# A two-layer graph network on one core: own pools for the staging tiles of the transformed taps, and another order for the first loads of the neighbour parts

## The chip, the cores and the metric

The kernel runs on one core of a Trainium2 chip. Its metric is the device time of one execution in microseconds. TensorE (PE), VectorE (DVE), ScalarE (ACT), GpSimd (POOL) and SyncE (SP) each work through their own list of instructions in order; SP and POOL also issue the DMAs, each to a queue of its own (q1 for SP, q0 for POOL in the profile).

## The reference, cut to what matters

128 graphs of 128 nodes with 256 channels go through two layers. The change lies in the first half of layer 0:

```
h = relu(layernorm(x))
xc = transpose(h)                                   # channels first
c  = relu(bn1(conv1x1(xc)))
c  = bn2(conv1d(c, conv2_w, 17 taps, pad 8))
x_conv = relu(c + xc)
s = h @ w_se.T + b_se                               # 3 channels
A = exp(-|s_n - s_m|^2) * adj
x_nmp = A @ relu(h @ w_msg.T + b_msg)               # the neighbour parts
layer 0 = GRU-like gates of (x_conv, x_nmp, h)
```

The convolution with 17 taps is done by a Fourier transform: the data and the taps are transformed, multiplied frequency by frequency, and transformed back.

## The kernel before, in words

All graphs are taken in 32 groups `q` of 4 graphs, and in two batches of 16 groups. The instruction order of every engine is written out by a small planner (`Order`, `Lane`) at build time: programs written as Python generators say at each `yield` how much time they think they have used, and the planner picks which one goes on. Nothing is reordered after that.

The stages that matter here, for the first batch, are these.

- `stage_a(q)` (lines 389 to 442) normalises a group, transposes it (`ph`, line 410), stores the transposed `hTa` into the DRAM tensor `hTd[q]` (line 415, a DMA that POOL issues), does the 1x1 convolution (`pc`, line 421) and the forward transform (`pf`, line 432) into the big on-chip tile `X`. `X` data is loaded by SP (`load_x`, line 381).
- `tap_weights()` (lines 459 to 499) runs beside it. It transforms the taps of the 17-tap convolution (`pw`, line 474), copies the results out of PSUM into a staging tile `ws` of 16 KB per partition (lines 479 and 481), and stores every `ws` into the DRAM tensor `wfd` with four DMAs of 320 KB issued by POOL (line 486). There are 16 `ws` tiles, named `ws{n}_{m}`, m even; the last four are `ws3_0`, `ws3_2`, `ws3_4`, `ws3_6`. They rotate through three buffers in the pool `tw`.
- When it is through, `tap_weights` closes `tw` (line 488) and opens the pools `wg`, `io`, `xe` and `fr` in the space that becomes free (lines 489 to 497). They have `reuse_waits="tile"`: a new tile waits for the last users of those old tiles whose bytes it covers, and for no others. `wmsg` and `bmsg`, the message weights and bias, are loaded at once by SP (lines 498 and 499).
- `early(q)` (lines 662 to 675) makes the neighbour part of group q: `load_n(q)` (lines 571 to 576) has SP load `hT` from `hTd[q]` and the adjacency `ad`; then `neighbours` (from line 608) does the embedding (`pse`, line 614), the messages (`pm`, line 630), the distances and the transposed adjacency (`pd`, lines 643 and 645) and the sum over neighbours (`px`, line 656).
- `stage_b(bat)` (lines 502 to 566) multiplies frequency by frequency (`pa`, `pb`, line 526). It starts with loads of `wf` from `wfd` (line 512), which SP issues behind the loads above, and which need every store of `wfd` to have landed. The neighbour parts are spread between its products.

On PE's list the end of `stage_a`, the first two neighbour parts, the messages of the third and then the first product of `stage_b` follow each other. On SP's list, after the last `x` load of the first batch (`xa15`), stand `wmsg`, `bmsg`, `hT0`, `adj0`, `hT1`, `adj1`, then `hT2`, `adj2` (which reuse buffers of group 0) and the first six loads of `wf`. On POOL's list stand the stores of `ws3_2`, of `hTd13`, of `ws3_4`, of `hTd14`, of `ws3_6`, of `hTd15`, and then the first store of a neighbour part.

In bytes per partition, from the built program: `tw` held `wse` at 23584, two `wt` tiles (taps as loaded) at 24128 and 40512, `wide` at 56896 and the three `ws` buffers at 58944, 75328 and 91712. The new pools put `hT0` at 55840 and `wmsg` at 80416.

Of the kernel before, what the change touches and what calls it, by code (L numbers as in the profile page):

```python
# [9 lines left out]
FP = mybir.dt.float32  # L10
# [5 lines left out]
B, N, D = 128, 128, 256  # L16
# [3 lines left out]
P = 128  # L20
# [187 lines left out]
def kernel(ctx: ExitStack, tc: tile.TileContext, x, adj, consts, vecs, w_se, conv1_w,  # L208
                    conv2_w, w_msg, b_msg, w_ih, w_hh, W1, W2, b2, fusion_w, out):
    nc = tc.nc  # L210
# [11 lines left out]
    hTd = [dr.tile([P, 2, 512], FP, name=f"hTd{q}") for q in range(NQ)]  # L222
# [10 lines left out]
    def c(name):  # L233
        a, b = CAT[name]
        return cst[:, a:b]
# [14 lines left out]
    def load_late():  # L250

        nc.sync.dma_start(out=fus, in_=fusion_w.partition_broadcast(P))
        nc.sync.dma_start(out=wse, in_=w_se.rearrange("(k p) o -> p k o", p=P))
        nc.sync.dma_start(out=cst[:, CFIRST:], in_=consts[:, CFIRST:])
# [76 lines left out]
    def fold_embedding():  # L331

        nc.vector.memset(wse9, 0.0)
        for role in range(3):
            nc.vector.tensor_copy(wse9[:, :, 3 * role:3 * role + 3], wse[:, :, :3])
        pbs = ptmp.tile([P, 512], FP, tag="tmp", name="pbs")
        nc.tensor.matmul(pbs[:, :1], c("sel"), v("b_se"), start=True, stop=True)
        bse = cp.tile([P, 1], FP, name="bse")
        nc.vector.tensor_copy(bse, pbs[:, :1])
        nc.vector.scalar_tensor_tensor(embb, emb[:, 4:8], bse, emb[:, 8:12],  # L340
                                       op0=ALU.mult, op1=ALU.add)
        yield 1.5, 0.0
# [26 lines left out]
    LATE, XA, MOM = {}, {}, {}  # L369
# [73 lines left out]


    mid, near = ExitStack(), ExitStack()
    tw = mid.enter_context(tc.tile_pool(name="tw", bufs=2))
    wse = tw.tile([P, 2, 67], FP, tag="wse", name="wse", bufs=1)
    wts = []

    def load_taps(n, *engines):  # L450

        wt = tw.tile([P, 16, D], FP, tag="wt", name=f"wt{n}")
        src = conv2_w.rearrange("(r n i) t o -> n t r i o", r=4, n=4)[n]
        for r in range(4):
            engines[r % len(engines)].dma_start(out=wt[32 * r:32 * r + 16], in_=src[:16, r])
        engines[0].dma_start(out=wt[16::32], in_=src[16])
        wts.append(wt)

    def tap_weights():

        yield 0.0, 16.0
        for n in range(4):
            for m in range(8):
                if m == (0 if n else 3) and n < 3:
                    load_taps(n + 1, nc.sync, nc.gpsimd)
                if (n, m) == (1, 3):
                    load_late()
                if m % 2 == 0:
                    ws = tw.tile([P, 4, 4, D], FP, tag="ws", name=f"ws{n}_{m}", bufs=3)
                pws = [(pgat if r < 3 else ptmp).tile([P, 2, D], FP, tag="gat" if r < 3 else "tmp",  # L470
                                                      name=f"pw{n}_{m}_{r}") for r in range(4)]
                for r in range(4):
                    rows = slice(32 * r, 32 * r + TAPS)
                    nc.tensor.matmul(pws[r][:F], c("tap")[rows], wts[n][rows, 2 * m:2 * m + 2],  # L474
                                     start=True, stop=True)
                i = m % 2 * 2
                for r in range(4):
                    if r < 2 or (r == 2 and m % 2):
                        nc.scalar.activation(ws[:F, r, i:i + 2], pws[r][:F], AF.Copy)
                    else:  # L480
                        nc.vector.tensor_copy(ws[:F, r, i:i + 2], pws[r][:F])
                yield 0.9, 2.2
                if m % 2:
                    for r in range(4):
                        i0 = 64 * r + 16 * n + 2 * (m - 1)
                        nc.gpsimd.dma_start(out=wfd[:, i0:i0 + 4], in_=ws[:F, r])
        yield from fold_embedding()
        mid.close()
        wg = ctx.enter_context(tc.tile_pool(name="wg", bufs=1, reuse_waits="tile"))
        LATE["wrz"] = wg.tile([P, 7, 3, D], FP, name="wrz")  # L490
        LATE["wn"] = wg.tile([P, 7, 2, P], FP, name="wn")
        LATE["wh"] = wg.tile([P, 7, 1, P], FP, name="wh")
        LATE["io"] = near.enter_context(tc.tile_pool(name="io", bufs=2, reuse_waits="tile"))
        LATE["xe"] = near.enter_context(tc.tile_pool(name="xe", bufs=1, reuse_waits="tile"))
        LATE["fr"] = near.enter_context(tc.tile_pool(name="fr", bufs=1, reuse_waits="tile"))
        LATE["wmsg"] = LATE["fr"].tile([P, 2, D], FP, name="wmsg")
        LATE["bmsg"] = LATE["fr"].tile([P, D], FP, name="bmsg")
        nc.sync.dma_start(out=LATE["wmsg"], in_=w_msg.rearrange("(k p) o -> p k o", p=P))
        nc.sync.dma_start(out=LATE["bmsg"], in_=b_msg.partition_broadcast(P))


    def stage_b(bat):
# [65 lines left out]

    EN, IN, IN2, X1, E_DONE, F_DONE = {}, {}, {}, {}, set(), set()

    def load_n(q):
        hT = LATE["io"].tile([P, 2, 512], FP, tag="hT", name=f"hT{q}")
        nc.sync.dma_start(out=hT, in_=hTd[q])
        ad = LATE["io"].tile([P, GB, N], FP, tag="adj", name=f"adj{q}")
        nc.sync.dma_start(out=ad, in_=adj[q * GB:(q + 1) * GB].rearrange("b n m -> n b m"))
        return hT, ad
# [85 lines left out]
    def early(q):  # L662

        while q not in A_DONE:
            yield 0.0, 0.5
        if q not in EN:
            EN[q] = load_n(q)
            yield 0.0, 6.0
        hT, ad = EN.pop(q)
        if q + 1 < NQ and q + 1 in A_DONE:  # L670
            EN[q + 1] = load_n(q + 1)
        xm = LATE["fr"].tile([P, 2, 512], FP, tag="xnmp", name=f"xnmp{q}", bufs=2)
        yield from neighbours(q, hT, ad, xm)
        nc.gpsimd.dma_start(out=xmd[q], in_=xm)
        E_DONE.add(q)
# [37 lines left out]
    def stage_c(q):  # L713
# [60 lines left out]
        for ps, i in ((p6, 5), (p5, 4)):  # L774
            part(ps, wrz, i, early, True, False)
            yield 1.75, 0.0
# [350 lines left out]
    load_xa(2)  # L1127
    fold()
    beside = Lane([tap_weights()] + [early(q) for q in range(NQ)])
    gates = Lane([fold_gates(), fold_fusion()], weight=0.5)  # L1130
    for bat, (during_a, during_b) in enumerate(((0.66, 0.5), (0.2, 0.65))):
# [60 lines left out]
```

## Time and profile before

| | |
|---|---|
| time, median of 3 runs | 2035.58 us (2028.67 to 2042.47) |
| the profiled execution's own time | 2034.12 us |
| its span, first to last instruction | 2032.3 us |
| PE busy | 1989.3 us, 98% of the span |
| DVE, POOL, ACT busy | 1285.2, 741.2 and 683.8 us |
| DMA | 281.91 MB, mean 139 GB/s |
| mean granted TensorE clock | 0.994 |

A busy PE is a PE with a matmul in it; the granted clock tells how fast it may run. In a timeline a line gives the start, the busy time, the engine, the source line, what is written and read, and in square brackets the idle time just before with what ended it. Stretches of time are given in microseconds from the span's start.

### The profile page before, as it was taken

What the parts mean: (1) busy time and instruction counts of PE and PEld (TensorE: products, weight loads), DVE (VectorE), ACT (ScalarE), POOL (GpSimd) and SP (SyncE); (2) the same over time, 40 slices, a digit from 0 to 9 for tenths busy, and PEclk for the clock granted to TensorE, in tenths of its full rate; (3) what the DMA queues carried; (4) which work ended last, traced back from release to release, by engine and by line L of the source; (5) the groups of instructions that cost most, each with busy time, mean ns of one, the idle gap of its engine ahead of it and who ended that gap; (6) DMA issues with size and microseconds to landing.
All of it is one profiled execution on the core that took longest, in us unless ns stands there. A gap on an engine that the chain in (4) does not pass through costs nothing.

```text
span 2032.3 us, 34053 instructions
## 1 busy us (share of the span) xinstructions
PE 1989.3 (98%) x12852; PEld 1653.7 (81%) x12852; DVE 1285.2 (63%) x2807; ACT 683.8 (34%) x1547; POOL 741.2 (36%) x898
## 2 busy tenths in 40 slices
PE   7998999999999999999999999999999999999998
PEld 5666888889888888778788878878888888878875
DVE  6774445785433566766775775677577757766643
ACT  4663222454222344232322322232233322232233
POOL 3542666332655022532333233224323323332330
PEclk9999999999999999999999999999999999999999
DMA  9987879744877633432322322322232323232121
GB/s 214 297 266 226 269 255 285 222 145 161 269 257 254 188 115 89 147 90 68 105 73 84 96 83 73 97 83 80 82 108 68 90 84 93 79 100 84 37 82 53
DMA packets 190266, 281.91 MB, mean 139 GB/s; under 512 B 23745, under 2 KB 143494, under 8 KB 190102
## 3 DMA queue, kind: packets, MB, share of 16 engines
q1 hardware_dynamic: 157062, 185.46, 31.5%
q0 software_dynamic: 32656, 93.98, 14.2%
q8 instruction: 102, 1.67, 0.4%
q14 instruction: 62, 0.51, 0.1%
q10 hardware_dynamic: 384, 0.28, 0.1%
HBM read 187.34 MB, written 92.27 MB: 138 GB/s over the span
## 4 chain that ended last, share of the span: by engine, by line
PE 90%; DVE 3%; issue 2%; DMA 2%; POOL 2%; ACT 1%; SPq 0%; POOLq 0%; DVEq 0%; ACTq 0%
PE p L741 41%; PE pa L526 7%; PE pm L630 5%; PE ph L1049 5%; PE pz L1058 5%; PE pc L421 4%; PE pb L526 3%; PE px L656 3%; PE pf L432 3%; PE pi L698 3%; PE po L887 1%; PE ph L410 1%; PE py L1032 1%; PE pw L474 1%; PE pse L614 1%
## 5 line engine op out<-in xcount | busy, mean ns | idle before, releaser
L867 POOL TENSOR_TENSOR hTc<-hTc,r 128x512 f32<-128x512 f32 x64 | 88.7, 1385 | 255.8 <-ACT r L864 255.8
L526 PE MATMUL pa<-wf,X 128*128 128x256 f32 x640 | 152.2, 381 | 0.0
L558 DVE SCALAR_TENSOR_TENSOR y<-pa,kk 128x512 f32<-128x512 f32 x78 | 53.8, 690 | 151.2 <-ACT kk L557 151.1
L896 POOL DMA_DIRECT2D out<-xt x128 | 72.0, 569 | 175.1 <-DVE xt L893 172.0
L741 PE MATMUL p<-th,wrz 128*128 128x256 f32 x512 | 134.6, 385 | 0.0
L741 PE MATMUL p<-tc,wrz 128*128 128x256 f32 x512 | 131.5, 379 | 0.0
L741 PE MATMUL p<-tm,wrz 128*128 128x256 f32 x512 | 131.4, 379 | 0.0
L526 PEld LDWEIGHTS pa<-wf,X 128*128 128x128 f32 x640 | 118.2, 190 | 16.1 <-issue 2.0
L421 PE MATMUL pc<-c1w,hTa 128*128 128x256 f32 x512 | 122.3, 386 | 1.9 <-DVE X L438 1.7
L630 PE MATMUL pm<-wmsg,hT 128*128 128x256 f32 x512 | 123.4, 387 | 0.0
L1051 ACT ACTIVATE hh<-ph,vec 128x96 f32<-128x96 f32 (+3 forms) x160 | 63.8, 401 | 140.8 <-PE ph L1049 131.7
L1049 PE MATMUL ph<-yz,w 128*128 128x96 f32 (+3 forms) x640 | 109.7, 325 | 1.0 <-issue 1.0
L421 PEld LDWEIGHTS pc<-c1w,hTa 128*128 128x128 f32 x512 | 95.0, 192 | 18.9 <-DVE h L424 4.8
L741 PEld LDWEIGHTS p<-th,wrz 128*128 128x128 f32 x512 | 94.6, 190 | 19.1 <-issue 7.4
L630 PEld LDWEIGHTS pm<-wmsg,hT 128*128 128x128 f32 x512 | 97.0, 193 | 16.1 <-issue 1.6
L710 ACT ACTIVATE xc<-xc,t_bn 128x256 f32<-128x256 f32 x128 | 58.0, 500 | 149.2 <-DVE xc L707 149.2
L741 PEld LDWEIGHTS p<-tm,wrz 128*128 128x128 f32 x512 | 97.4, 190 | 13.1
L1058 PE MATMUL pz<-hh,w 128*128 128x96 f32 (+3 forms) x640 | 107.3, 322 | 0.0
L1049 PEld LDWEIGHTS ph<-yz,w 128*128 128x128 f32 x640 | 88.4, 194 | 21.3 <-issue 14.5
L741 PEld LDWEIGHTS p<-tc,wrz 128*128 128x128 f32 x512 | 95.0, 190 | 11.6
L1058 PEld LDWEIGHTS pz<-hh,w 128*128 128x128 f32 x640 | 86.6, 191 | 17.7
L741 PE MATMUL p<-hTc,wrz 128*128 128x256 f32 x384 | 98.9, 380 | 0.0
(200 smaller groups left out, 4579.5 us busy)
## 6 DMA issues: line engine op xcount, KB each, us to landing
wf<-wfd SPq DMA_DIRECT2D x160, 256.0 KB
wfd<-ws POOLq DMA_DIRECT2D x64, 320.0 KB, 9.2
yd<-y POOLq DMA_DIRECT2D x80, 256.0 KB, 4.1
yt<-yd SPq DMA_DIRECT2D x64, 320.0 KB
w<-in_W SPq DMA_DIRECT2D x40, 512.0 KB
xa<-in_x SPq DMA_DIRECT2D x128, 128.0 KB
hTd<-hTa POOLq DMA_DIRECT2D x32, 512.0 KB, 6.5
hT<-hTd SPq DMA_DIRECT2D x32, 512.0 KB
```

Of the source, the lines that this page charges most:

```text
L421: nc.tensor.matmul(pc[:, i], hT[:, k, (2 * h + i) * N:(2 * h + i + 1) * N], c1w[:, k], start=(k == 0), stop=(k == 1))
L432: nc.tensor.matmul(pf[:, i, :F * NB], h1[:, 2 * h + i, k * P:(k + 1) * P], fwd, start=True, stop=True)
L526: nc.tensor.matmul(ps, xk(k), WF[f][:, k, s], start=(k == 0), stop=(k == 1))
L630: nc.tensor.matmul(pm[:, i], hT[:, k, j * N:(j + 1) * N], LATE["wmsg"][:, k], start=(k == 0), stop=(k == 1))
L656: nc.tensor.matmul(px[:, dc, i], msgs[h][:, i, dc * P:(dc + 1) * P], aT[:, 2 * h + i], start=True, stop=True)
L698: nc.tensor.matmul(pi[w * WIDE:(w + 1) * WIDE, :, :, n].rearrange("p k g c -> p g k c"), inv[:F, o:o + WIDE], yt[:, n // 2::2].rearrange(" ...
L741: nc.tensor.matmul(ps[:, m], w[:, i, k, m * P:(m + 1) * P], factor(i, x, t), start=first and j == 0, stop=last and j == len(n) - 1, skip_g ...
L867: nc.gpsimd.tensor_sub(d, d, r[:, dc])
L896: nc.gpsimd.dma_start(out=out[q * GB + j, WIDE:].rearrange("(t n) c -> n t c", n=WIDE), in_=xt[j * WIDE:(j + 1) * WIDE, 1:4])
L1049: nc.tensor.matmul(ph, w1[:, k, m * P:(m + 1) * P], yz[:, k, :, o:o + n], start=(k == 0), stop=(k == 1))
L1051: nc.scalar.activation(hh[:, m], ph, AF.Relu, bias=v("b1", g * 4 + m))
L1058: nc.tensor.matmul(pz, w2[:, g, m, cc * P:(cc + 1) * P], hs[g][:, m], start=(m == 0), stop=(m == 3))
```

## The change

The 16 `ws` tiles no longer rotate through three buffers of `tw`. They get three pools of one buffer each, `tws0`, `tws1` and `tws2`, that lie ahead of `tw`; number k of them (0 to 15) goes to pool `(0, 2, 1)[k % 3]`, so a tile still follows the one three before it. `wh` is made 512 bytes per partition longer, which makes the pool `wg` exactly as long as two `ws` buffers. The load of `hT0` is issued ahead of those of `wmsg` and `bmsg`, and the adjacency's behind them; the planner's time for the first neighbour part is kept by an extra `yield`.

```diff
     mid, near = ExitStack(), ExitStack()
+    tws = [mid.enter_context(tc.tile_pool(name=f"tws{i}", bufs=1)) for i in range(3)]
     tw = mid.enter_context(tc.tile_pool(name="tw", bufs=2))
...
                 if m % 2 == 0:
-                    ws = tw.tile([P, 4, 4, D], FP, tag="ws", name=f"ws{n}_{m}", bufs=3)
+                    ws = tws[(0, 2, 1)[(4 * n + m // 2) % 3]].tile([P, 4, 4, D], FP, tag="ws",
+                                                                   name=f"ws{n}_{m}")
...
-        LATE["wh"] = wg.tile([P, 7, 1, P], FP, name="wh")
+        LATE["wh"] = wg.tile([P, 8, 1, P], FP, name="wh")[:, :7]
         LATE["io"] = near.enter_context(tc.tile_pool(name="io", bufs=2, reuse_waits="tile"))
         LATE["xe"] = near.enter_context(tc.tile_pool(name="xe", bufs=1, reuse_waits="tile"))
         LATE["fr"] = near.enter_context(tc.tile_pool(name="fr", bufs=1, reuse_waits="tile"))
+        load_h(0)
         LATE["wmsg"] = LATE["fr"].tile([P, 2, D], FP, name="wmsg")
         LATE["bmsg"] = LATE["fr"].tile([P, D], FP, name="bmsg")
         nc.sync.dma_start(out=LATE["wmsg"], in_=w_msg.rearrange("(k p) o -> p k o", p=P))
         nc.sync.dma_start(out=LATE["bmsg"], in_=b_msg.partition_broadcast(P))
+        EN[0] = load_n(0)
...
+    HT = {}
+
+    def load_h(q):
+        HT[q] = LATE["io"].tile([P, 2, 512], FP, tag="hT", name=f"hT{q}")
+        nc.sync.dma_start(out=HT[q], in_=hTd[q])
+
     def load_n(q):
-        hT = LATE["io"].tile([P, 2, 512], FP, tag="hT", name=f"hT{q}")
-        nc.sync.dma_start(out=hT, in_=hTd[q])
+        if q not in HT:
+            load_h(q)
+        hT = HT.pop(q)
         ad = LATE["io"].tile([P, GB, N], FP, tag="adj", name=f"adj{q}")
...
         while q not in A_DONE:
             yield 0.0, 0.5
+        if q == 0:
+            yield 0.0, 6.0
         if q not in EN:
             EN[q] = load_n(q)
             yield 0.0, 6.0
```

## The prediction

> **What bounds the kernel now.** The page first: PE is busy for 1989.3 of 2032.3 us, so all its idle time together is 43.0 us, and a change that adds no work for another engine can win only out of that, and out of matmuls that run at less than the full clock.
>
> ```profile
> PE 1989.3 (98%) x12852; PEld 1653.7 (81%) x12852; DVE 1285.2 (63%) x2807; ACT 683.8 (34%) x1547; POOL 741.2 (36%) x898
> ```
>
> Next PE's timeline around the place that the change touches, from the end of stage A to the first product of stage B. The one long hole is ahead of the first `pse`: 7.78 us, ended by the load of `hT`.
>
> ```profile
> 160.94 3.62 PE L421 MATMUL pc<-c1w,hTa 128*128 128x256 f32 x16
> 172.34 1.08 PE L614 MATMUL pse<-hT,wse 128*32 128x128 f32 x16 [7.78 <-DMA hT<-hTd]
> 173.35 5.41 PE L630 MATMUL pm<-wmsg,hT 128*128 128x256 f32 x16
> ...
> 184.31 0.65 PE L614 MATMUL pse<-hT,wse 128*32 128x128 f32 x16
> 184.88 3.72 PE L630 MATMUL pm<-wmsg,hT 128*128 128x256 f32 x16
> ```
>
> The same 16 + 16 matmuls take longer for group 0 than for group 1. The table of stretches says why: the granted clock (the number after POOL's) falls to about 0.7 in the second half of the hole and stays there for the first matmuls after it. From 200 to 355 us PE is busy throughout.
>
> ```profile
> 164.60:168.00 3.40, 0.00 (x0) 0.00 (x0) 0.69 (x1) 0.63 (x1) 0.00 (x0) 1.00 0.86 237
> 168.00:172.30 4.30, 0.00 (x0) 0.00 (x0) 0.00 (x0) 0.00 (x0) 0.00 (x0) 0.73 0.80 256
> 172.30:180.00 7.70, 7.66 (x47) 6.04 (x48) 1.81 (x3) 2.61 (x6) 0.00 (x0) 0.71 0.28 92
> 225.00:355.00 130.00, 130.00 (x785) 112.66 (x784) 62.17 (x102) 35.98 (x98) 83.02 (x103) 1.00 0.85 272
> ```
>
> Then the chain of waits through this window. It runs over the last store of the taps, then the load of `hT`, then PE. So the end of the kernel hangs on it.
>
> ```profile
> 159.06 8.69 DMA wfd<-ws
> ...
> 167.90 4.31 DMA hT<-hTd
> ...
> 172.34 1.08 PE pse L614 x16
> 173.42 5.35 PE pm L630 x16
> ...
> 184.38 0.57 PE pse L614 x16
> 184.95 3.67 PE pm L630 x16
> ```
>
> Last, SP's own timeline. Its `x` loads end at 135.41 (126.56 + 8.85); then it stands still until 161.17, held by a store of `ws3_4`, and again until 167.90, held by the stores of `ws3_6`.
>
> ```profile
> 126.56 8.85 SPq L381 DMA_DIRECT2D xa<-in_x  x4
> 161.17 0.38 SPq L498 DMA_DIRECT2D wmsg<-in_w_msg  x1
> 161.60 1.87 SPq L499 DMA_DIRECT2D bmsg<-in_b_msg  x1
> 167.90 0.34 SPq L573 DMA_DIRECT2D hT<-hTd  x1
> 168.29 0.47 SPq L575 DMA_DIRECT2D adj<-in_adj  x1
> ```
>
> **What the Trainium skill says.** "DMA: Bandwidth & Descriptors", section "Anatomy of one DMA — SWDGE (gpsimd) path": DMA engines do not wait on semaphores, the issuing sequencer does. The trace agrees: SP issued nothing for 25.8 us, though the adjacency and the bias behind the waiting load are plain inputs. Same page, "Queues, rings and completion order": each DMA engine goes round-robin between the queues that have work. From 165 to 166 us the trace has 65 packets of q0 and 54 of q1, about one to one by the profile's count. "TensorE: Matmul & The Clock Gate", section "Part 1: The HAM clock gate": after an idle window of about 3.4 us the clock is halved, and some 3.4 us of work bring it back. The trace agrees: 1.00 for the first 3.4 us of the hole, 0.73 after, and group 0's `pm` at 5.35 against 3.67 us.
>
> **The change part by part.** In the built program the instructions of PE, ACT, DVE and POOL stand in the order they had, one for one; on SP's list one load moves, `hT0`, two places up. What the edits do is in the addresses and the waits.
>
> *The pools.* The three `ws` buffers now lie at 23584, 39968 and 56352; `wg`, now 32768 bytes, covers the first two exactly and `hT0` and the adjacency lie at 56352 and up, over `tws2`, whose last tile is `ws3_2`. In the built waits `hT0` asks for the stores of `ws3_2` and no longer for those of `ws3_6`. `wmsg` and `bmsg` lie over a `wt` tile, whose last reader is a matmul of the third of the four sets of taps, long past. `adj0`, `hT1` and `adj1` ask for nothing else new. `ef`, `lr` and `xnmp` lose a wait for a store. The stores of `ws3_2` are POOL's four from 144.14 to 147.48; those issued last landed 5.4 to 6.5 us after issue, the last one issued at about 147.0, so `hT0` can go at 147.0 + 6.5 = 153.5 us, 14.4 us earlier than 167.90. The others follow at SP's pace (0.34 + 0.38 + 1.87 + 0.47 + 0.34 + 0.43 us): all six issued by about 157.5.
>
> *The move of hT0.* It is passed by nothing that had been ready: ahead of it stands `xa15`, issued by 135.41. `wmsg` and `bmsg` now stand behind its wait, but go earlier than before (154 against 161.17). Had `wmsg` stayed first, nothing much would differ, since it waits for nothing; the move gives `hT0` the head of q1.
>
> *When the data is there.* The six loads now run against the stores. I work out the service from the rates of before. `wmsg`, issued at 161.17, got its first packets near 164.5, so 3 us pass first; `hT0` starts at 156.5. It has 128 rows of 4 KB; q0 alone moved 162 packets in 154 to 156 us, 81 per us, so shared one to one it takes 128 / 40 = 3.2 us, to 159.7. `wmsg` has 256 rows of 1 KB, at 54 per us 4.7 us, to 164.4; `bmsg`, 128 rows, to 166.8. `adj0` has 512 rows of 512 bytes; q0's stores last until about 168.5, so some 90 go at 54 per us, and the other 420 alone at over 270 per us (q1's rate from 170 to 171) in 1.6 us, to about 170. PE needs them at 164.56 (`pse`), 165.1 (`pm`), DVE the bias at 167.0, PE the adjacency at 164.56 + 0.57 + 3.67 + 0.45 = 169.2. What is late is the adjacency, by 0.8 us. Bounds: 0, if q0 leaves more room (its share is only 72 to 80% from 156 to 160 us), and 4.5, if q1 gets nothing until q0 drains near 167 and `hT0` and `wmsg` (0.79 MB at 0.28 MB per us) come at 169. Below nothing is excluded: the idle time cannot be less than none. I take 0.8.
>
> *The clock.* With the hole under 3.4 us PE stays at full speed: 1.08 - 0.57 = 0.51 us on `pse` and 5.35 - 3.67 = 1.68 us on `pm`, together 2.19. Bounds 0 (a hole of 4 us or more remains) and 2.19.
>
> *What is late next.* The `wf` loads. They stand behind `hT2` and `adj2`, which need group 0's `pm` and `pd`, so they follow PE: issued at 180.28 before, about 171 after. New is that the stores of `ws3_6` and `hTd15`, sharing the engines with 1.9 MB of loads, land later than at 167.75 and 169.2: the same bytes are moved in sum, so near 171 to 172. The first product stood at 196.71, would stand near 187.5, and its loads took some 8 us from 180.28; 172 + 8 = 180, so about 7 us of cover are left. If that cover were gone, each us would be lost to PE. POOL may wait longer ahead of `hTd15`'s store; behind it stands only the store of a neighbour part, due after 176. `wh`'s extra bytes and the extra yield cost no instruction.
>
> The sum against the profiled execution (2034.12 us, span 2032.3): 7.78 + 2.19 - 0.8 = 9.2 us less, 2024.9. All of PE's later list follows with no hole until 355 us, and SP's waits there are for PE, so the lead is carried. The median of the runs, 2035.58, lies 1.46 above the profiled one: 2035.58 - 9.2 = 2026.4.
>
> **The rivals.**
> *The hole only moves.* The loads are starved by the stores and PE waits inside group 0 for weights or adjacency. For: SP's queue got almost nothing from 161 to 165 us while q0 was at 93% and more. Against: q1 got 54 packets per us from 165 on, and the loads now have 11 us of lead. With 4.5 us of hole left and half of the clock's gain: 7.78 - 4.5 + 1.1 = 4.4 less, 2031.2.
> *The lead is lost later.* PE is early by 9 us and some later transfer, not tied to PE, takes it back (the chain has loads of `xa` near 355 us). Against: those loads go when PE frees their buffers. Time 2035.6.
> *Slower: the taps' stores are pushed back.* The mechanism is one: the early loads take bandwidth from `ws3_6` and `hTd15`, the first `wf` load is held, and PE stands ahead of the first product. It decides from the point where the last of these stores lands after 196.7 - 8 = 188.7, 21 us later than before; landing at 195 would cost 6 us, 2042. Against: only 1.9 MB of loads stand before them, 7 us at 0.28 MB per us.
> *More than worked out*, some 20 us or more (2013): nothing in the profile speaks for it but the spread of the runs.
>
> **How the numbers follow.** Forecast 0.66; hole moves 0.18; lead lost 0.08; slower 0.05; more 0.03. The runs of before spread over 13.8 us, more than the effect, so the range takes the unknown costs (gain 4.4 to 10) and some 7 us of spread on either side: 2017 to 2036. About 1% (20 us) is what a measurement of this kernel can tell from no change. The forecast and the next two cases lie within it, and most of the slower one: faster 0.04, same 0.93, slower 0.03.
>
> **What would show it.** Right: SP issues `hT` near 153.5 and `wmsg`, `bmsg`, adjacency right behind; no idle of more than 1 us ahead of `pse`; clock 1.00 from 160 to 200; `pm` of group 0 at 3.7 us; the first product near 187.5, and the rest 9 us earlier. Wrong: a new wait of PE ahead of `pm` or `pd`; a first product not earlier than 196; `ws3_2`'s stores landing well after 153.5; or a lead at 200 us that is gone at 700.

## The result, and the profile after

| | before | after |
|---|---|---|
| median of 22 runs each | 2034.51 us (2027.82 to 2042.47) | 2027.93 us (2023.49 to 2036.02) |
| the profiled execution's own time | 2034.12 us | 2029.67 us |
| its span | 2032.3 us | 2027.9 us |
| mean granted TensorE clock | 0.994 | 0.996 |

The ratio of after to before is 0.9971, with a 95% interval of 0.9959 to 0.9984: 5.9 us less (2034.51 x 0.0029), between 3.3 and 8.3. That is within 1%, as forecast. The forecast gain, 9.2 us, is a ratio of 0.9955, which lies just outside the interval: the sign and the place were right, the size was too large by some 3 us.

The page's row of engines shows that PE's work is the same; what changed is its idle time, 38.8 us (2027.9 - 1989.1) against 43.0.

```profile
PE 1989.1 (98%) x12852; PEld 1651.6 (81%) x12852; DVE 1285.4 (63%) x2807; ACT 683.7 (34%) x1547; POOL 742.3 (37%) x898
```

PE's timeline of the kernel after, around the place of the change. The line numbers have moved: `pse` is now line 625, `pm` 641.

```profile
158.69 3.62 PE L421 MATMUL pc<-c1w,hTa 128*128 128x256 f32 x16
165.69 1.04 PE L625 MATMUL pse<-hT,wse 128*32 128x128 f32 x16 [3.39 <-DMA hT<-hTd]
168.88 5.54 PE L641 MATMUL pm<-wmsg,hT 128*128 128x256 f32 x16 [2.15 <-DMA wmsg<-in_w_msg]
...
179.97 0.65 PE L625 MATMUL pse<-hT,wse 128*32 128x128 f32 x16
180.54 3.72 PE L641 MATMUL pm<-wmsg,hT 128*128 128x256 f32 x16
```

The hole of 7.78 us is not gone here: 3.39 us are left of it, and a second of 2.15 us stands ahead of `pm`, for the message weights. Group 0's `pm` takes 5.54 us where group 1's takes 3.72. The granted clock (the number after POOL's in the table of stretches) falls to half at 165.80, as the first hole ends, and stays there for 6.8 us, as long as before:

```profile
164.60:168.00 3.40, 1.04 (x16) 0.61 (x16) 0.00 (x0) 1.23 (x4) 0.00 (x0) 0.68 1.00 322
168.00:172.30 4.30, 3.42 (x8) 2.82 (x9) 0.42 (x1) 0.28 (x1) 0.00 (x0) 0.50 0.35 116
```

The DMA share, the last but one number, is 1.00 in the first stretch, against 0.86 before. SP's timeline shows `hT` issued at 152.29 instead of 167.90, as the change intends. The loads behind it follow slowly: the issue of `wmsg` takes 3.92 us where it took 0.38.

```profile
152.29 0.35 SPq L579 DMA_DIRECT2D hT<-hTd  x1
152.75 3.92 SPq L501 DMA_DIRECT2D wmsg<-in_w_msg  x1
156.72 3.00 SPq L502 DMA_DIRECT2D bmsg<-in_b_msg  x1
159.77 1.97 SPq L586 DMA_DIRECT2D adj<-in_adj  x1
```

By the profile's account the chain of waits no longer runs over a store of the taps, but over the load of `wmsg`, 16 us from issue to landing:

```profile
152.75 16.00 DMA wmsg<-in_w_msg
168.88 5.55 PE pm L641 x16
```

So this one profile shows the rival "the hole only moves". Whether it is typical had to be tried.

### The profile page after: what moved, and what is told of

It is laid out like the page before. It is cut to its first block, busy times and chain, and to the rows that moved or that the text cites. A ratio compares the mean times of both kernels' runs of the same rounds, so it can differ in the third digit from the quotient of the medians.

```text
span 2027.9 us, 34053 instructions
## 1 busy us (share of the span) xinstructions
PE 1989.1 (98%) x12852; PEld 1651.6 (81%) x12852; DVE 1285.4 (63%) x2807; ACT 683.7 (34%) x1547; POOL 742.3 (37%) x898
## 4 chain that ended last, share of the span: by engine, by line
PE 91%; DVE 3%; issue 2%; DMA 1%; POOL 1%; ACT 1%; SPq 0%; ACTq 0%; DVEq 0%; POOLq 0%
PE p L754 41%; PE pa L530 7%; PE pm L641 5%; PE ph L1062 5%; PE pz L1071 5%; PE pc L421 5%; PE pb L530 3%; PE pf L432 3%; PE pi L711 3%; PE px L667 3%; PE pw L476 2%; PE ph L410 1%; PE po L900 1%; PE py L1045 1%; PE pse L625 1%
## 5 line engine op out<-in xcount | busy, mean ns | idle before, releaser
L909 POOL DMA_DIRECT2D out<-xt x128 | 72.0, 569 | 175.3 <-DVE xt L906 172.2
L530 PEld LDWEIGHTS pa<-wf,X 128*128 128x128 f32 x640 | 118.1, 190 | 16.2 <-issue 2.0
```

The lines of the kernel that those rows point to most:

```text
L530: nc.tensor.matmul(ps, xk(k), WF[f][:, k, s], start=(k == 0), stop=(k == 1))
L909: nc.gpsimd.dma_start(out=out[q * GB + j, WIDE:].rearrange("(t n) c -> n t c", n=WIDE), in_=xt[j * WIDE:(j + 1) * WIDE, 1:4])
```

## The experiments

All ratios are to the kernel before, with their 95% intervals. Each is to runs of the kernel before that were taken beside it; their median was 2034.51 us for after, 2033.52 for `again`, `pools_only`, `order_only` and `fill_before`, 2035.66 for `last_store_early` and `pools_pf`, and 2036.21 for `pools_2` and `early_io`, so medians of different lines can't be compared. Since the ratios differ by a few tenths of a per cent, each profile also gets a local measure: the time from the end of the last `pc` of stage A to the first product `pa`. PE's work there is the same in all kernels but `fill_before`, which has 6.2 us more, and `pools_pf`, which has less, so otherwise the differences are PE's waits and its clock. "hT0" gives the landing times of its sixteen parts, the fifteenth and the last, from the trace's records of landings.

| kernel | ratio | median us | last `pc` to first `pa`, us | hT0: 15th part, last part |
|---|---|---|---|---|
| before | 1 | 2034.51 | 164.6 to 196.7: 32.1 | 172.2, 172.2 |
| before_2 | one run | 2041.40 | 168.3 to 200.4: 32.0 | 174.9, 175.1 |
| after | 0.9971 (0.9959 to 0.9984) | 2027.93 | 162.3 to 192.4: 30.1 | 160.1, 165.6 |
| again (the same) | 0.9978 (0.9966 to 0.9990) | 2028.71 | 161.9 to 185.7: 23.9 | 159.1, 159.9 |
| after_3 (the same) | one run | 2023.14 | 163.2 to 187.3: 24.2 | 160.4, 161.0 |
| after_4 (the same) | one run | 2027.22 | 162.3 to 187.9: 25.7 | 159.7, 160.0 |
| order_only | 1.0001 (0.9989 to 1.0013) | 2033.29 | 161.9 to 191.1: 29.2 | 167.0, 167.1 |
| pools_only | 0.9968 (0.9957 to 0.9979) | 2027.36 | 162.1 to 184.3: 22.2 | 159.5, 160.5 |
| pools_2 (the same) | 0.9958 (0.9946 to 0.9971) | 2025.71 | 163.0 to 185.1: 22.2 | 160.5, 160.7 |
| fill_before | 0.9993 (0.9982 to 1.0004) | 2031.69 | 161.1 to 190.1: 29.1, more work | 167.4, 167.8 |
| last_store_early | 0.9983 (0.9967 to 0.9999) | 2031.45 | 166.4 to 195.8: 29.5 | 164.8, 168.5 |
| pools_pf | 1.0034 (1.0019 to 1.0049) | 2042.40 | 164.5 to 185.9: 21.4, less work | 164.5, 168.8 |
| early_io | 0.9958 (0.9942 to 0.9974) | 2024.77 | 163.4 to 185.5: 22.2 | 146.6, 146.6 |

**The changed kernel again, three times.** `again` was timed; `after_3`, `after_4` and `before_2` are one execution each, for their profiles.

> The changed kernel itself, a second profile. In its first profile 15 of the 16 parts of the load of hT0 had landed by 160.1 us and the last at 165.6, and PE lost 3.4 us ahead of pse and 2.2 ahead of pm. Theory A (one DMA engine happens to lag in a run, by some 5 us): in another profile the lag stands at other places, the hole can be under 2 us and then pm of group 0 takes 3.7 us. Theory B (the loads are always that late behind the taps' stores): the same hole of 5 to 6 us, pm at 5.4 to 5.5 us. Time: ratio 0.997 either way, give or take 0.0015.

> The changed kernel for a third profile: PE lost 5.5 us ahead of pse and pm in the first, with one part of sixteen of each load late by 5 us, and 2.2 us ahead of the adjacency's transposes in the second. Theory A (one DMA engine that lags in some executions): again no lag over 2 us, and 0 to 2.5 us lost at the adjacency; or a lag of 3 to 6 us as in the first. Theory B (a lag in every execution): cannot hold after the second profile unless the lag comes back with the same size and place.

> The changed kernel, a fourth profile, to see how often the lag comes: with it 29 to 30 us from the last pc of group 15 to the first product, without it 23.9 to 24.2. From three profiles, one with and two without, I expect no lag in two of three cases.

> The kernel before once more, for a second profile. The forecast took the hole ahead of the first pse from one profile, 7.78 us; the runs order_only and fill_before, which load hT0 behind the same stores, lost 5.3 and 7.0 us there. Theory A (the hole of the first profile was on the long side, typical is 5.5 to 7): hole 5.5 to 7 us, and stage A ends (last pc of group 15) near 162 us instead of 164.6. Theory B (7.8 is what the kernel before has): 7.5 to 8 us.

Before's two profiles agree in the sum, 32.1 and 32.0 us, but not in its parts. In `before_2` the hole is 6.84 us, and the clock is at half for 10.2 us instead of 6.8, so that `pm` takes 6.23 us:

```profile
175.19 1.08 PE L614 MATMUL pse<-hT,wse 128*32 128x128 f32 x16 [6.84 <-DMA hT<-hTd]
176.20 6.23 PE L630 MATMUL pm<-wmsg,hT 128*128 128x256 f32 x16
```

The four of after do not agree: 30.1, 23.9, 24.2 and 25.7. In the last three `hT0` is complete when PE wants it, and no hole is left ahead of `pse` or `pm`. What is left stands at the adjacency, as in PE's timeline of `again`:

```profile
161.81 0.65 PE L625 MATMUL pse<-hT,wse 128*32 128x128 f32 x16
162.39 3.72 PE L641 MATMUL pm<-wmsg,hT 128*128 128x256 f32 x16
...
168.71 0.66 PE L656 MATMUL pd<-cst,adj 128*128 128x128 f32 x4 [2.17 <-DMA adj<-in_adj]
```

`after_3` has 2.48 us there and `after_4` 2.36. In `after_4` 3.4 us at half the clock follow from 170.2, and the next 16 `pf` take 4.05 us where they take 2.42 in `after_3`:

```profile
169.27 0.66 PE L656 MATMUL pd<-cst,adj 128*128 128x128 f32 x4 [2.36 <-DMA adj<-in_adj]
169.76 4.05 PE L432 MATMUL pf<-cst,h 128*128 128x160 f32 x16
```

The first profile of after differs in this: fifteen of the sixteen parts of `hT0` had landed at 160.1, near the 159.7 of the forecast, and the last came at 165.6. "DMA: Bandwidth & Descriptors", section "Why a DMA increments its semaphore by 16 and not by 1", says that up to 16 engines take part and finish independently, and that only the full count means that the data is there. The trace agrees: `pse` starts at 165.69, with the sixteenth part. The mean of the four local measures is 25.9 us, 6.1 under before's 32.1, and the times say 5.9; with four profiles that spread over 6 us, so close a match is partly luck.

**Each half of the change alone.** `pools_only` has the new pools and `wh`, and the loads in the old order. Against the kernel after:

```diff
-        load_h(0)
...
-        EN[0] = load_n(0)
...
-        if q == 0:
-            yield 0.0, 6.0
```

> The pools alone; the first loads stay in the order wmsg, bmsg, hT0, adj0. wmsg and bmsg wait for nothing of the stores now and go near 136 us, hT0 as in the changed kernel near 153. If the pools are what counts, the ratio is that of the changed kernel, 0.995 to 0.998. If the early weights take the wait of PE for wmsg away, it is a little better than the changed kernel (by up to 2 us); if the order matters as the change has it, it is worse by 1 to 3 us.

`order_only` has the old pools and the new order. Against the kernel after:

```diff
-    tws = [mid.enter_context(tc.tile_pool(name=f"tws{i}", bufs=1)) for i in range(3)]
...
-                    ws = tws[(0, 2, 1)[(4 * n + m // 2) % 3]].tile([P, 4, 4, D], FP, tag="ws",
-                                                                   name=f"ws{n}_{m}")
+                    ws = tw.tile([P, 4, 4, D], FP, tag="ws", name=f"ws{n}_{m}", bufs=3)
...
-        LATE["wh"] = wg.tile([P, 8, 1, P], FP, name="wh")[:, :7]
+        LATE["wh"] = wg.tile([P, 7, 1, P], FP, name="wh")
```

> The order alone, with the staging tiles in the old pool. hT0 then waits for the last store of ws3_6 (167.8 us before), and wmsg, bmsg and adjacency stand behind it instead of 6.5 us ahead. Theory (the pools are what counts): no gain, rather 1 to 2 us slower than before, since wmsg now comes after hT0: ratio 1.000 to 1.001. Rival (the order brings the gain): 0.997.

The pools carry the whole gain in time: 0.9968, and `order_only` 1.0001. PE's timeline of `pools_only` has no hole at all at this place:

```profile
162.04 0.65 PE L623 MATMUL pse<-hT,wse 128*32 128x128 f32 x16
162.62 3.72 PE L639 MATMUL pm<-wmsg,hT 128*128 128x256 f32 x16
166.71 0.66 PE L654 MATMUL pd<-cst,adj 128*128 128x128 f32 x4
```

SP's timeline tells why. In the old order `wmsg` does not stand behind the wait of `hT0`. It goes at 129.91, while the taps are still being made, and the adjacency goes at 151.91, next after `hT0`. It has landed at 161.3, where it landed at 168.7 to 170.3 in the three profiles of after without the late part:

```profile
129.91 1.90 SPq L500 DMA_DIRECT2D wmsg<-in_w_msg  x1
...
151.51 0.34 SPq L577 DMA_DIRECT2D hT<-hTd  x1
151.91 1.90 SPq L584 DMA_DIRECT2D adj<-in_adj  x1
```

In `order_only` `hT` still waits for the stores of `ws3_6`; it goes at 163.53, and PE's timeline keeps a hole of 5.30 us and a slow `pm`:

```profile
167.19 1.08 PE L623 MATMUL pse<-hT,wse 128*32 128x128 f32 x16 [5.30 <-DMA hT<-hTd]
168.20 4.98 PE L639 MATMUL pm<-wmsg,hT 128*128 128x256 f32 x16
```

Its local measure is 2.9 us better than before, and the time shows nothing of it. In this profile the last store of `ws3_6` landed 7.0 us after its issue; with the old pools and the old order (before, `before_2`, `fill_before`) it took 8.7, 8.5 and 8.1. The weights no longer run beside it, but one profile does not show that this is the reason.

**`pools_only` again, as `pools_2`.** To see whether it has after's scatter.

> The pools alone a second time: its first profile lost nothing between the end of stage A and the first product (22.2 us). hT0 is still loaded at 151 to 153 us beside the stores, so an execution in which one DMA engine lags by 5 us would lose 3 to 4 us ahead of pse and the clock's 2 us; weights and bias are in place in any case. Without a lag 22.2 us again. Ratio 0.9965 to 0.9975.

It shows none: 22.2 us a second time, and no wait for a load. Two profiles do not exclude a late part, and `pools_pf` below, with the same pools and order, has one. In time after (0.9971, 0.9978) and the old order (0.9968, 0.9958) are not told apart, since the intervals overlap; the profiles do tell them apart, four against two, by 1.7 us at least.

**The clock by itself.** Before, with fourteen matmuls into an unused PSUM tile in the hole (28 instructions, 6.21 us).

```diff
+        if q == 0:
+            fl = ptmp.tile([P, 2, D], FP, tag="tmp", name="fl")
+            for _ in range(14):
+                nc.tensor.matmul(fl[:, 0], c1w[:, 0, :P], c1w[:, 0], start=True, stop=True)
         pse = ptmp.tile([P, 512], FP, tag="tmp", name=f"pse{q}")
```

> The kernel before with 14 added matmuls (28 instructions, about 6 us at full clock) on constant operands ahead of the first pse, in the hole of 7.8 us; their result is not used. It prices the clock by itself. If the slow matmuls after the hole come of the hole, the clock stays at 1.00, pm of group 0 takes 3.7 instead of 5.4 us and the time falls by 2.2 us (ratio 0.9989). If not, pm stays at 5.4 us and the time is the same.

```profile
160.93 6.21 PE L614 MATMUL fl<-c1w 128*128 128x256 f32 x28
167.90 0.65 PE L618 MATMUL pse<-hT,wse 128*32 128x128 f32 x16 [0.77 <-DMA hT<-hTd]
168.48 3.72 PE L634 MATMUL pm<-wmsg,hT 128*128 128x256 f32 x16
```

PE waits for `hT` just as before, but `pse` takes 0.65 us and `pm` 3.72: the clock's loss is caused by the hole, and keeping PE busy in it takes it away. Of the 3.1 us by which the local measure fell, 1.0 is a shorter stand (from the last `pc` to `pse` 6.8 us against 7.8) and 2.1 the clock (from `pse` to the first product 22.2 against 24.4). The time's interval, -3.7 to +0.8 us, holds both -2.2 and 0, so the time alone settles nothing.

**Less traffic against the loads.** After, with the last tile's stores left out at their place; the rows of another tile are stored in that part of `wfd` 30 us earlier, so the bytes in sum stay.

```diff
-                if m % 2:
+                if m % 2 and (n, m) != (3, 7):
...
+                        if (n, m) == (2, 7):
+                            i0 = 64 * r + 16 * 3 + 12
+                            nc.gpsimd.dma_start(out=wfd[:, i0:i0 + 4], in_=ws[:F, r])
```

> The changed kernel, with the four stores of ws3_6 left out at their place and rows of the same number and size stored from ws2_6 some 30 us earlier instead, so the last group of transformed taps is wrong; bytes and instructions are the same. 1.3 MB of stores less lie beside the loads of hT0, wmsg, bmsg and adj0. If those loads are held by sharing with the stores, the adjacency lands some 3 us earlier against the end of stage A and PE waits for it under 0.5 us (2.2 in the second profile of the changed kernel), from the last pc of group 15 to the first product 22 to 22.5 us; the extra stores can cost stage A 0 to 4 us. If a load has its own fixed time instead, the wait at the adjacency stays near 2 us.

Inconclusive. Stage A ended at 166.4, 3 to 4.5 us later than in after's profiles, and one part of `hT0` lagged again, by 3.7 us (164.8, 168.5). PE had no wait for the adjacency, but 2.28 us ahead of `pse` and 2.00 ahead of `pm`. So the lag does not need the stores of `ws3_6`; what the loads gain without them can't be read from this.

**A cover for the late loads.** `pools_only` with the neighbour parts held on the planner until stage A has ended, which puts the last `pf` ahead of `pse`.

```diff
+        while q == 0 and BQ - 1 not in A_DONE:
+            yield 0.0, 0.2
```

> The pools without the new order of loads, and with the forward transforms of group 15 (pf, 16 instructions, 2.2 us) ahead of the first pse on PE's list instead of behind pd, so that PE has them to do while loads arrive. It also moves the neighbour parts by one place between the products of stage B. If lagging loads cost the pools' kernels 1 to 3 us in the mean, ratio 0.9955 to 0.9965 against 0.9968 for the pools alone; if the first wf loads, which are needed some 8 us sooner in this order, come late, PE waits 1 to 4 us ahead of the first product and the ratio is 0.998 to 0.999.

Slower than before: 0.34% (0.19 to 0.49). Its local measure, 21.4 us, is not a gain: the `px` of the second neighbour part and the `pse` and `pm` of the third, 6.1 us in `pools_only` (178.17 to 184.28), come behind the first product here. One part of `hT0` lagged by 4.3 us; PE waited 1.65 us ahead of `pse` and 2.73 for the adjacency, and the clock was at half for 3.4 us. By the pages PE is idle for 45.9 us of the whole span (2042.2 - 1996.3) against 32.6 in `pools_only` (2021.5 - 1988.9), and busy for 7.4 us more. The neighbour parts have other places between the products, so that more of them fall into the stage A of the second batch; how the one leads to the other was not followed. The stretches at the beginning of that stage, `pools_pf` first and `pools_only` second, whose work is not quite the same, show PE idle for 5.2 of 57.1 us at a clock of 0.96, against 2.7 of 59.1 at 1.00:

```profile
342.90:400.00 57.10, 51.90 (x335) 45.12 (x334) 42.59 (x115) 25.49 (x60) 18.11 (x19) 0.96 0.69 203
```

```profile
340.90:400.00 59.10, 56.36 (x369) 50.22 (x369) 46.51 (x125) 27.26 (x61) 17.27 (x20) 1.00 0.68 207
```

**The loads earlier still.** After, with the buffers of `hT` and the adjacency moved, so that they lie over a tile of taps that is free sooner and wait for no store of `ws3_2`.

```diff
-        LATE["io"] = near.enter_context(tc.tile_pool(name="io", bufs=2, reuse_waits="tile"))
         LATE["xe"] = near.enter_context(tc.tile_pool(name="xe", bufs=1, reuse_waits="tile"))
+        LATE["xe"].tile([P, 1160], FP, name="gap")
+        LATE["io"] = near.enter_context(tc.tile_pool(name="io", bufs=2, reuse_waits="tile"))
```

> The changed kernel with the buffers of hT, adjacency, message weights and bias moved up by 16.9 KB, over a buffer of the taps as loaded (last read at about 120 us) instead of the staging tile of ws3_2. On SP's list nothing moves, but all six loads can go right behind the last x load, near 135 us, 20 us before the changed kernel's, and PE needs them at about 162. If what the changed kernel loses against the forecast is late landing (a DMA engine that lags by 5 us in some executions, and the adjacency by 2.2 to 2.5 us in the others), nothing is waited for: last pc of group 15 to first product in 22.2 us as in pools_only, against 23.9 to 30.1 in three profiles of the changed kernel and 32.0 in two of the kernel before, and the ratio is 0.995 to 0.9965. If the lost part lies elsewhere (given back after 200 us), the ratio stays at 0.997 to 0.998 in spite of the 22.2 us. If the loads now hold the taps' stores and stage A, the last pc ends 1 to 3 us later than the 162 to 163 us of the changed kernel.

`hT` is issued at 135.16 and has landed at 146.6, 17 us ahead of PE; no part of it lags in this profile, and PE runs through. The lines are from SP's and PE's timelines:

```profile
135.16 3.18 SPq L580 DMA_DIRECT2D hT<-hTd  x1
```

```profile
163.28 0.64 PE L626 MATMUL pse<-hT,wse 128*32 128x128 f32 x16
163.86 3.72 PE L642 MATMUL pm<-wmsg,hT 128*128 128x256 f32 x16
```

0.9958, and the same 22.2 us as `pools_only`. This and the old order with the new pools both beat the kernel before; neither is shown in time to beat the kernel after.

## Why the prediction was right, and where its size was off

*The pools: shown.* `hT0` asks for the stores of `ws3_2`, and goes at 152.29 (forecast 153.5). With the old pools it goes at 163.53 in the new order, and at 163.88, 167.90 and 171.54 in the old (`fill_before`, before, `before_2`).

*The two large terms: shown as what there is to win.* 7.78 for the hole and 2.19 for the clock off before's 32.15 us give 22.18; `pools_only`, `pools_2` and `early_io`, where nothing is late, show 22.2 each. The split was that of one profile: in `before_2` it is 6.84 and about 3.0 (32.0 - 22.2 - 6.84). The clock's term is also shown alone, by `fill_before`.

*The clock's limit of 3.4 us: did not hold.* "With the hole under 3.4 us PE stays at full speed", said the prediction. After's hole of 3.39 us was followed by the whole loss, and `after_4`'s of 2.36 us by 3.4 us at half the clock, while holes of 2.17 and 2.48 us cost nothing. "TensorE: Matmul & The Clock Gate", section "Part 1: The HAM clock gate", calls the window of 3.4 us free-running. The traces agree: in their records of the granted clock every stretch between two changes is a whole number of times 3.413 us long (after: 44, 2 and 247 times). Counted back from the changes, `after_4`'s hole lies in one such window, in which PE was busy for only 1.05 of 3.41 us, and the next window has half the clock:

```profile
166.82:170.23 3.41, 1.05 (x12) 0.96 (x8) 0.67 (x3) 1.22 (x5) 0.00 (x0) 1.00 0.93 341
170.23:173.64 3.41, 3.41 (x14) 3.35 (x14) 1.00 (x5) 1.07 (x4) 0.00 (x0) 0.50 0.76 237
```

The hole of `after_3`, though longer, is split over two windows with 2.14 and 2.19 us of work, and the clock stays. So its length alone does not tell what a hole costs; where it falls in the windows fits what was seen here. In before the first whole window without work ends at 169.98, so the clock fell there, 5.4 us into the hole and not after 3.4.

*The step that failed is "When the data is there": 0.8 us forecast, 1.7, 2.0, 3.5 and 7.9 us measured* (each local measure less 22.2, the clock's share included), 3.8 on average. These 3.0 us are what lacks of the 9.2. Three things are in it.

First, the order of the loads. The prediction said "Had `wmsg` stayed first, nothing much would differ". In the profiles it does differ: 22.2 us with the old order, 23.9 to 30.1 with the new. "`wmsg` and `bmsg` now stand behind its wait, but go earlier than before" compared with the old pools; compared with the new pools and the old order they go 18 to 23 us later, into a stretch in which the DMA engines are full (share 0.96 from 152 to 162 us in after, 0.68 from 140 to 150), and the adjacency stands behind them. Even so it was issued at 155.5 to 156.5 us and came at 168.7 to 170.3 in the three profiles without a lag, as forecast (153.5 + 0.34 + 0.38 + 1.87 = 156.1, and 170). But PE came for it at 166.5 to 167.8, not at 169.2, as stage A ended 1.4 to 2.7 us sooner than in before's profile. It did so in `fill_before` and `order_only` too, so this does not need the change: the sum was made on a single profile, in which PE's arrival was later than in these.

Second, the lag of one of the sixteen parts, which the sum had no term for. In one profile of four it left 5.5 us of holes and, with them, the clock's loss. There SP's pace slipped too: it had been taken from before, where `wmsg`, `bmsg` and the adjacency took 0.38, 1.87 and 0.47 us to issue; after has 3.92, 3.00 and 1.97, so "all six issued by about 157.5" became 166.3 (164.64 + 1.68). In the other three it was 160.2 to 160.5.

Third, the clock after short holes, as above: `after_4` lost some 1.5 us more to it than `after_3`.

*The rival "the hole only moves"*, given 0.18, is what the first profile of after shows (3.39 and 2.15 us left, and all of the clock's loss). It is one case of four and not the rule.

*"The lead is lost later": falls.* From the first product to the last matmul before takes 1829.4 and 1832.9 us, after 1829.2, 1830.5, 1827.8 and 1831.3, `pools_only` 1830.9 and `pools_2` 1825.9. The means are 1831.1 for before, 1829.7 for after and 1828.4 for the other two, so the lead at the first product is kept, as far as profiles of one kernel that spread by up to 5 us can tell.

*The slower rival*, the taps' stores pushed back until the first `wf` is late: falls. No profile of after or `pools_only` has a wait of PE ahead of the first product. The one kernel that became slower, `pools_pf`, has none there either.

*The median.* The forecast of 2026.4 came within 1.5 us of the measured 2027.93 partly by luck: it was built on a median of three runs, 2035.58, and that of 22 is 2034.51. From there the sum gives 2025.3, and 2.6 us lack.

What stays open: why one part lags, how often it does so in before, and whether the order alone, behind the new pools, can be seen in time.

## What to carry to other kernels

When a load waits for space, look at whose bytes it lies over: moving buffers so that the first load covers the tile that is free soonest took away a whole wait, with not one instruction changed. On a queue in order, put loads in the order in which their space is free, and no free load behind one that waits: here the load that was held back went into a busier stretch, which cost 1.7 us and more in these profiles, though the times do not show it. A local measure between two fixed points of the same engine told kernels apart that about 20 runs each could not; but the work between the points must be the same, and several profiles are needed, since one of after's four showed another mechanism than the rest.

## What the runs showed of the hardware that was not expected

- One part of sixteen of a load came 3.7 to 5.5 us after the others in 3 of the 8 profiles in which `hT0` was loaded beside the stores under the new pools (after, `last_store_early`, `pools_pf`); in after, POOL's DMAs that landed between 157 and 173 us had the same lag, 4.7 to 5.6 us (`hTd13`: 152.5 and 157.3). The whole load waits for it. The kernel before has it too, where nothing waited for it: in its profile POOL's stores that landed between 119 and 143 us had a last part 4.2 to 6.0 us behind the fifteenth. With 17 us in hand, as in `early_io`, a lag of that size could do nothing.
- SP's issue of a DMA took 0.33 to 0.5 us in some places and 1.7 to 4.8 in others, mostly while POOL's stores were under way too. For `wmsg` in after the trace puts 3.6 us down to a matmul of PE; but the old one that it asks for was done by 129.91, since the same load at the same address went then in `pools_only`. What makes an issue long was not tried by itself.
- The clock goes by windows of 3.41 us that do not begin with a hole, and a window need not be idle throughout to be followed by half the clock: 1.05 us of work in it did not keep the clock (`after_4`), 1.41 (before, 163.2 to 166.6 us) and 1.59 (`again`, 166.9 to 170.3) did. By the profile's count of work this is no sharp limit: in `pools_only` a window with 1.95 us of work, from 16.2, was followed by half the clock, and in before one that was busy throughout, up to 1019.9. What decided there was not followed.
- After's two holes, 3.39 and 2.15 us with 1.04 us of work between, cost as much of the clock as before's single one of 7.78: `pm` took 5.54 and 5.41 us.
